# Attention and routed experts on one core: divisions one tile later, the clears begun by GpSimd, the last row cut six to two

## The chip, the cores and the metric

The kernel runs on one core of one Trainium2 chip. A core has five engines with a queue of instructions each: TensorE (PE; its weight loads are PEld in the profile), VectorE (DVE), ScalarE (ACT), GpSimd (POOL) and the sync engine (SP). DMA transfers are begun from such a queue and carried out by 16 DMA engines beside them. The metric is the device time of one execution in microseconds; the median of six executions is what counts.

## The reference

The input is `x` of 8 rows (batch entries) of 1024 tokens with 128 features, in float32. One layer with two residual steps is computed:

```
x = x + attention(layernorm(x)) @ Wo      # 16 heads of 8, each token sees the last 64 tokens
x = x + moe(layernorm(x)) + bias          # 8 experts of width 512, top 2, capacity 2048
```

The attention is a sliding window: token `l` attends to the tokens `l-63` to `l`, with a softmax over them. The second step routes each token to the two of 8 experts with the largest router probability. Each expert takes at most 2048 tokens in the order of the tokens, runs `gelu(t @ w1) @ w2` on them, and the result, times the router's probability, is added to the token's row.

## The kernel before

The work has two phases. **The first** (0 to about 493 us) does the attention, the norms and the routing, and writes each token's normalized features, its two probabilities, its first expert's code and its index into `xb`, a table in DRAM with 8 x 2048 slots of 132 words. **The second** (about 493 us to the end) loads each expert's slots (`load_e`), transposes them (L1283), multiplies by `w1` (L1294) and `w2` (L1305), scales (L1310) and adds the result to the output rows by an indirect DMA (L1315).

The first phase walks over 64 tiles, `i = 8 * b + j`: row `b` of 8, tile `j` of 8 with 128 tokens. In iteration `i` of the loop at L1165 the order of the code is: one clear of `xb` (below), `scores` of tile `i + 2`, what was left of the plan of tile `i - 1` (`behind`), `attend` of tile `i - 1`, `probs` of tile `i`, the plan of tile `i`, and the `late` steps of tile `i`. TensorE, VectorE, ScalarE and GpSimd run in this order, written by hand; the sync engine's order is set by the framework.

- `scores` (L526): TensorE makes the scores (L543, L559), VectorE takes their maxima over 768 columns (L567) and two differences (L575). The score buffers in PSUM are three, shared with `probs`, so a late L567 keeps TensorE from L604 or L612 of the next `probs`.
- `probs` (L591): scores again, transposed, with the maxima subtracted (L604 or, in the first tile of a row, L612; then L621, L628), then two exponentials on ScalarE (L634).
- `attend` (L640): the products with the values and, beside them, the sums of the exponentials (L649), copied out by ScalarE to `sums` (L657).
- `Context` (L662): sums and products of a group of tiles go from `sums` to the layout of the next product by DMAs on the sync queue: four for the divisors `den` (L678), four for `ctx` (L680). Then `scale` (L701) inverts the divisors of a tile (L706, VectorE) and multiplies (L707). `steps` says how many tiles after the copy each call runs. The groups of a row are tiles 0 to 3 (`few`: divisors inverted in a smaller layout through DRAM, L675 to L698, multiplied three tiles later), 4 to 5 and 6 to 7; in rows 6 and 7 they are pairs, and the last tile is alone.
- `Piece` (L752) is the rest of a token's way: `out` (projection by `Wo`, L783, residual L788, router logits L789), `stats` and `root` (layer norm, L377 to L405), `softmax`, `exp`, `apply`, `choose` 0 and 1 (top 2), `count` (two matmuls, L860), `place` (slot numbers, L872 to L881), `slots` (which hangs two scatters per tile into a list), and `keep` (adds the bias on GpSimd, L811, and stores the rows by the sync queue, L812).
- `put(n)` (L899) takes `n` scatters from that list: each is an indirect DMA begun by GpSimd (L905) that writes 128 rows of 528 bytes into `xb`.
- `first` (L926) does the first layer norm of a row two rows ahead; `turn`, `queries`, `keys`, `values` (L434 to L492) project the next row, and `spread` (L494) lays it out by DMAs.
- `clears` (L310): sixteen DMAs of 528 KB from a tile of zeros into `xb`, begun by the sync engine (L316), one in each of iterations 1 to 13 and then up to two, each behind the last matmul of `probs` of the tile before. The scatters come after all of them.

The plan (`at`, L921, the loop at L974 and `half`, L1023) says in which tile each step of a row's `Piece` and of the next rows runs. The routing of row `b - 1` runs during row `b`. Row 6 is cut into two pieces of four tiles. So is row 7 (`piece`, L1056): `go(ends[k], n)` runs the next `n` steps of a piece, after the loop mostly (L1222 to L1231). There, `mark` (L1234) is a small GpSimd instruction behind the scatters before the last five, and `stay_awake(38)` gives TensorE 38 matmuls that nobody reads (L169), begun after `mark`, until the second phase's first slots arrive.

## Time and profile before

| What | us |
|---|---|
| Median of 6 runs | 762.42 (760.38 to 768.49) |
| The profiled execution's own time | 758.78 |
| Its span, first to last instruction | 756.70 |
| First phase's loop, first L634 to 440.0 | 414.23, TensorE busy 354.93 |
| 440.0 to the first L1283 at 493.34 | 53.34, TensorE busy 16.14 |
| 493.34 to the end | 263.36, TensorE busy 240.64 |

The profile is that of one execution. The page gives, for each engine, its busy time, the chain of work that ended last, and the groups of instructions by source line, with their count, busy time, mean duration in ns and the idle time of the engine just before them, with what ended most of it. The trace behind it can be asked for stretches, waits and the order of time. In the order of time a line has: start, us, engine, line, operation, output and input, count, and in brackets the idle time before it with what ended it. `SPq` is the sync engine's queue: its time is the time to begin a DMA, not that of the transfer. In a table of stretches come start and end, length, the busy time of PE, PEld, DVE, ACT and POOL with their instructions, the granted TensorE clock as a share of full speed, the share of DMA time and GB/s.

### The profile page before, as it was taken

How to read it: one execution, taken by the hardware profiler on the slowest of the kernel's cores; microseconds unless marked ns; L12 is line 12 of the kernel's file. 1: busy time of each engine (PE TensorE's matmuls, PEld its weight loads, DVE VectorE, ACT ScalarE, POOL GpSimd, SP SyncE). 2: the span in 40 equal slices, each digit the busy share in tenths (PEclk: the TensorE clock that was granted, in tenths of full speed). 3: DMA queues.
4: the chain of work that ended last, by engine and by line, in shares of the span. 5: the costliest groups of instructions: out<-in, count | busy, mean ns of one | idle time of the engine just before them, and what ended most of it. 6: DMA issues, size and time to landing. Idle time of an engine off the chain costs nothing.

```text
span 756.7 us, 21773 instructions
## 1 busy us (share of the span) xinstructions
PE 633.4 (84%) x8777; PEld 469.7 (62%) x8777; DVE 393.3 (52%) x1229; ACT 363.1 (48%) x637; POOL 358.4 (47%) x353
## 2 busy tenths in 40 slices
PE   8898697899999989999977640599999999999990
PEld 6444454555556545555544430589999999898990
DVE  6675596797896978977889673221111111111010
ACT  5465367467666565665654520023444444443430
POOL 7000000133434334524414356548778787787876
PEclk9999899899999999999999875699999999999996
DMA  2544445333343434333332111246456365463333
GB/s 77 164 136 134 150 156 170 117 100 118 101 127 107 140 112 137 112 102 93 101 100 70 59 49 51 61 124 114 51 106 109 44 123 94 52 120 34 36 32 30
DMA packets 78307, 73.99 MB, mean 98 GB/s; under 512 B 13907, under 2 KB 63928, under 8 KB 77312
## 3 DMA queue, kind: packets, MB, share of 16 engines
q1 hardware_dynamic: 55296, 55.59, 23.1%
q0 software_dynamic: 22528, 16.74, 15.7%
q8 instruction: 69, 1.13, 0.7%
q14 instruction: 30, 0.25, 0.1%
q10 hardware_dynamic: 384, 0.28, 0.1%
HBM read 19.14 MB, written 30.28 MB: 65 GB/s over the span
## 4 chain that ended last, share of the span: by engine, by line
PE 43%; DVE 19%; ACT 10%; issue 9%; POOL 6%; SPq 5%; DMA 5%; another core or an unknown queue 0%; POOLq 0%; DVEq 0%; ACTq 0%
PE yp L1305 12%; PE hp L1294 12%; ACT pr L634 6%; DVE mx L567 5%; PE av L649 5%; POOL out_dram L1315 4%; PE t L621 4%; SPq L678 3%; ACT mxt L586 2%; DVE den L706 2%; DMA den<-sums 2%; PE xt L1283 2%; DMA ctx<-sums 1%; PE awake L169 1%; PE t L604 1%
## 5 line engine op out<-in xcount | busy, mean ns | idle before, releaser
L1315 POOL DMA_INDIRECT out_dram<-ye,dest x128 | 197.4, 1542 | 66.0 <-issue 27.7
L905 POOL DMA_INDIRECT xb<-xn,si x128 | 125.6, 981 | 212.0 <-PE s L559 61.8
L634 ACT ACTIVATE pr<-t 128x1024 f32<-128x1024 f32 x128 | 123.7, 1018 | 69.0 <-PE t L628 63.5
L1305 PEld LDWEIGHTS yp<-w,hT 128*128 128x128 f32 x1024 | 124.1, 192 | 8.4 <-ACT hT L1298 5.3
L1305 PE MATMUL yp<-w,hT 128*128 128x128 f32 x1024 | 125.3, 275 | 4.0 <-DVE ye L1310 3.3
L567 DVE TENSOR_REDUCE mx<-s 128x8 f32<-128x768 f32 x128 | 116.1, 949 | 15.9 <-PE s L559 15.9
L1294 PE MATMUL hp<-xts,w 128*128 128x256 f32 (+1 forms) x528 | 121.8, 373 | 0.3 <-DVE xts L1285 0.3
L1310 DVE TENSOR_TENSOR ye<-yp,gt 128x256 f32<-128x256 f32 (+1 forms) x66 | 27.1, 415 | 161.3 <-PE yp L1305 125.4
L1298 ACT ACTIVATE hT<-hp 128x512 f32<-128x512 f32 x128 | 76.3, 597 | 68.7 <-PE hp L1294 64.2
L1294 PEld LDWEIGHTS hp<-xts,w 128*128 128x128 f32 x528 | 93.3, 190 | 10.3 <-DVE xts L1285 0.6
L621 PE MATMUL t<-qbd,kt 32*128 32x256 f32 x1024 | 78.2, 397 | 0.0
L649 PE MATMUL av<-pr,vbd 128*32 128x128 f32 x2016 | 69.4, 278 | 8.2 <-ACT vbd L482 2.7
L657 ACT COPY sums<-av 128x512 f32<-128x512 f32 x63 | 36.9, 585 | 82.0 <-PE av L649 74.1
L811 POOL TENSOR_TENSOR x<-x,bias_sb 128x256 f32<-128x256 f32 x28 | 20.6, 750 | 113.2 <-ACT xn L417 113.0
L649 PEld LDWEIGHTS av<-pr,vbd 128*32 128x32 f32 x2016 | 52.1, 110 | 28.9 <-ACT mxt L586 13.3
L1285 ACT COPY xts<-xt 128x256 f32<-128x256 f32 (+1 forms) x57 | 21.0, 368 | 87.2 <-PE xt L1283 82.7
L559 PE MATMUL s<-kbd,qt 32*32 32x384 f32 x2048 | 59.9, 493 | 0.9 <-DMA kbd<-kt 0.9
L621 PEld LDWEIGHTS t<-qbd,kt 32*128 32x128 f32 x1024 | 54.5, 194 | 3.3 <-issue 1.6
L604 PE MATMUL t<-i,mt 32*128 32x256 bf16 x448 | 30.1, 277 | 17.0 <-DVE mx L567 15.5
L706 DVE RECIPROCAL den<-den 128x128 f32<-128x128 f32 x39 | 36.9, 947 | 12.7 <-DMA den<-sums 12.6
L586 ACT COPY mxt<-pm 128x512 bf16<-128x512 bf16 x64 | 37.8, 591 | 1.5 <-PE pm L584 1.5
L543 PE MATMUL s<-ms,i 32*128 32x256 bf16 x256 | 28.0, 276 | 11.4 <-ACT pr L634 6.4
(180 smaller groups left out, 730.4 us busy)
## 6 DMA issues: line engine op xcount, KB each, us to landing
xb<-zeros SPq DMA_DIRECT2D x16, 528.0 KB
xe<-xb SPq DMA_DIRECT2D x7, 1056.0 KB
vbd<-vbd SPq DMA_DIRECT2D x32, 192.0 KB
kbd<-kt SPq DMA_DIRECT2D x62, 72.0 KB
qbd<-qt SPq DMA_DIRECT2D x64, 64.0 KB
out_dram<-x SPq DMA_DIRECT2D x32, 128.0 KB
w<-in_L_ffn_w_dram SPq DMA_DIRECT2D x16, 256.0 KB
x<-in_L_attn_x_dram SPq DMA_DIRECT2D x22, 128.0 KB
```

What stands on the lines that cost most here:

```text
L559: done = nc.tensor.matmul(place(g, slice(32 * blk, 32 * (blk + 1))), lhsT=qt[quad(g), q0 : q0 + 32], rhs=kbd[quad(g), :, c0 + 32 * blk : c ...
L567: nc.vector.tensor_reduce(out=part_of(mx, 0)[:, 2 * u : 2 * u + 2], in_=units[u][:, :, 0 : 4 * KB].rearrange("p g (r k) -> p g r k", r=4), ...
L586: nc.scalar.copy(mxt.rearrange("p r w q -> p (r w q)"), pm.rearrange("p r q -> p (r q)"))
L621: nc.tensor.matmul(units[g // 2][:, g % 2, w], lhsT=kt[quad(g), q0 : q0 + P], rhs=qbd[quad(g), :, c0 : c0 + 64], start=False, stop=False, ...
L634: nc.scalar.activation(pr[:, 2 * u : 2 * u + 2], units[u], AF.Exp)
L649: last = nc.tensor.matmul(av[quad(g), k, :, w], lhsT=pair_values(vbd, 2 * j + w, g, k), rhs=pr[:, g, w, 2 * k : 2 * k + 2, :], start=True, ...
L706: nc.vector.reciprocal(den, den)
L905: ins = nc.gpsimd.indirect_dma_start(out=xb[:, :], out_offset=bass.IndirectOffsetOnAxis(ap=slot, axis=0), in_=row, in_offset=None, bounds_ ...
L1294: nc.tensor.matmul(hp[:, c], lhsT=ws[e][0][:, (c0 + c) * P : (c0 + c + 1) * P], rhs=xt, start=True, stop=True,)
L1298: nc.scalar.activation(hT[:, c0 : c0 + per], hp, AF.Gelu_apprx_tanh)
L1305: nc.tensor.matmul(yp[:, k, :], lhsT=hT[:, c, k * P : (k + 1) * P], rhs=ws[e][1][:, c, :], start=c == 0, stop=c == NC - 1,)
L1315: add = nc.gpsimd.indirect_dma_start(out=acc, out_offset=bass.IndirectOffsetOnAxis(ap=dests[e][:, n : n + 1], axis=0), in_=ye[:, k, :], in ...
```

## The change

The division of a tile (`scale`) runs two tiles after the copy for the first of a pair and three for the second, instead of one and two, and in rows 6 and 7 two for both. The steps that need it, and what follows them, move by a tile: the last projection, its statistics and root from tile 3 to 4, softmax to `place` from `n = b * NJ + 4` to `n = b * NJ + 5` on, while `slots` and the first `keep` stay in their tile. `values` of the next row goes from tile 4 to 5, behind `queries`; the statistics of the row after next from tile 1 to tile 7 of the row before. The last row's pieces have six and two tiles instead of four and four; the steps after the loop are shared out anew, and `mark` stands ahead of the last piece's `count`, `place` and `slots`. The sixteen clears are begun by GpSimd, from a tile of zeros of half the size, so with twice the runs of half the length.

```diff
-        zeros = c1.tile([P, 4, W], F32, tag="zeros", name="zeros")
+        zeros = c1.tile([P, 2, W], F32, tag="zeros", name="zeros")
...
-            n: c1.tile([P, E * n], F32, tag=f"goon{n}", name=f"go_on{n}") for n in (2, 4, 8)
+            n: c1.tile([P, E * n], F32, tag=f"goon{n}", name=f"go_on{n}") for n in (2, 4, 6, 8)
...
-                into = nc.sync.dma_start(
-                    out=to.rearrange("p (m k) -> p m k", m=NS // 8),
-                    in_=bc_mid(zeros.rearrange("p n d -> p (n d)"), NS // 8),
+                into = nc.gpsimd.dma_start(
+                    out=to.rearrange("p (m k) -> p m k", m=NS // 4),
+                    in_=bc_mid(zeros.rearrange("p n d -> p (n d)"), NS // 4),
                 )
...
-                return (
-                    (1 + t * (self.b != 6), partial(self.scale, t)) for t in range(self.n)
-                )
+                return ((2 + t * (self.b < 6), partial(self.scale, t)) for t in range(self.n))
...
-                at(b, 3, of, *f, "out", 6, 2)
+                at(b, 4, of, *f, "out", 6, 2)
             if b + 1 < B:
-                at(b, 4, values, b + 1, 0)
                 at(b, 4, turn, b + 1, 1)
                 at(b, 5, queries, b + 1, 1)
+                at(b, 5, values, b + 1, 0)
...
-                at(b, 1, first, b + 2, "stats")
+                at(b - 1, 7, first, b + 2, "stats")
...
-            at(b, 3, of, *f, "stats", range(2, 4))
-            at(b, 3, of, *f, "root", nc.vector)
-            n = b * NJ + 4
+            at(b, 4, of, *f, "stats", range(2, 4))
+            at(b, 4, of, *f, "root", nc.vector)
+            n = b * NJ + 5
             for t, what, *args in (
                 (n, "rooted"), (n, "softmax"),
                 (n + 1, "choose", 0),
                 (n + 2, "choose", 1),
-                (n + 5, "slots"),
-                (n + 5, "keep", (0,)), (n + 5, "keep", (2,)),
-                (n + 6, "keep", (4,)), (n + 7, "keep", (6,)),
+                (n + 4, "slots"),
+                (n + 4, "keep", (0,)), (n + 5, "keep", (2,)),
+                (n + 6, "keep", (4,)), (n + 6, "keep", (6,)),
...
-        half(6, 0, (53, 2), (54, 3), (56, 5), (57, 2), (58, 3))
-        half(6, 4, (57, 2), (58, 2), (59, 1), (60, 5), (61, 2), (62, 3))
+        half(6, 0, (53, 2), (55, 3), (56, 5), (57, 2), (58, 3))
+        half(6, 4, (57, 2), (59, 3), (60, 5), (61, 2), (62, 3))
...
-        ends = [piece(0, 4), piece(4, 8)]
+        ends = [piece(0, 6), piece(6, 8)]
         at(7, 5, go, ends[0], 2)
-        at(7, 7, go, ends[0], 8)
-        at(7, 7, go, ends[1], 2)
+        at(7, 7, go, ends[0], 9)
...
-        for which, n in ((0, 2), (1, 2), (0, 2)):
+        for which, n in ((0, 2), (1, 3), (0, 2)):
             go(ends[which], n)
         put(2)
         for n in (2, 1, 2):
             put(2, go(ends[1], n))
         put(len(puts), go(ends[1], 2))
+
+        mark = nc.gpsimd.memset(nothing, 0.0)
         go(ends[1], 3)
-        put(3)
+        put(len(puts))
         go(ends[0], 1)
         go(ends[1], 1)
-
-        put(max(0, len(puts) - 5))
-        mark = nc.gpsimd.memset(nothing, 0.0)
-        put(len(puts))
         after(stay_awake(38).ins, mark.ins)
```

## The prediction

> **What bounds the kernel now.** I read the page first, then a table of stretches cut where the first tile of each row begins its exponentials, then the list of waits, then the order of time around the two longest gaps and around the change of phase. The page gives three lines.

> ```profile
> PE 43%; DVE 19%; ACT 10%; issue 9%; POOL 6%; SPq 5%; DMA 5%; another core or an unknown queue 0%; POOLq 0%; DVEq 0%; ACTq 0%
> L706 DVE RECIPROCAL den<-den 128x128 f32<-128x128 f32 x39 | 36.9, 947 | 12.7 <-DMA den<-sums 12.6
> xb<-zeros SPq DMA_DIRECT2D x16, 528.0 KB
> ```

> The chain that ends last is TensorE's for less than half; VectorE, the sync queue and DMA hold 29% of it. VectorE stands idle before the division (L706) until the sums' DMA lands. The table of stretches (start:end, length, then busy time by engine) for rows 0, 1 and 3:

> ```profile
> 25.77:82.23 56.46, 45.63 (x892) 25.88 (x893) 34.75 (x97) 29.19 (x47) 0.00 (x0) 0.96 0.41 138
> 82.23:136.94 54.71, 45.78 (x864) 27.60 (x864) 39.45 (x120) 31.94 (x55) 1.49 (x2) 0.94 0.48 164
> 187.32:236.47 49.15, 44.82 (x867) 26.75 (x866) 40.62 (x123) 31.71 (x55) 18.66 (x20) 1.00 0.37 112
> ```

> TensorE is busy about 45 us in each. Rows 0 and 1 last 5 to 7 us longer, and GpSimd does next to nothing in them. By the starts of L634, the whole excess lies in one step: from the last tile of the row to the first of the next it takes 13.26 us (68.97 to 82.23) and 12.33 us (124.61 to 136.94), where rows 2 to 5 take 6.72, 6.73, 6.91 and 6.72. The order of time inside the first:

> ```profile
> 70.61 0.55 SPq L316 DMA_DIRECT2D xb<-zeros  x1
> 71.26 3.02 SPq L678 DMA_DIRECT2D den<-sums  x4
> 73.28 0.69 DVE L707 TENSOR_TENSOR ctx<-ctx,den 128x512 f32<-128x512 f32 x1 [4.61 <-DMA den<-one_910i]
> 74.32 2.50 SPq L680 DMA_DIRECT2D ctx<-sums  x4
> 75.55 0.95 DVE L706 RECIPROCAL den<-den 128x128 f32<-128x128 f32 x1 [1.58 <-DMA den<-sums]
> 78.14 0.29 DVE L707 TENSOR_TENSOR ctx<-ctx,den 128x128 f32<-128x128 f32 x1 [1.64 <-DMA ctx<-sums]
> 78.35 1.81 DVE L567 TENSOR_REDUCE mx<-s 128x8 f32<-128x768 f32 x2
> 79.36 0.51 PE L612 MATMUL t<-i,mt 32*128 32x128 bf16 x10 [6.61 <-DVE mx L567]
> 82.23 1.94 ACT L634 ACTIVATE pr<-t 128x1024 f32<-128x1024 f32 x2 [9.05 <-PE t L628]
> ```

> The maxima (L567) for scores made by 71.2 start at 78.35, because three VectorE instructions ahead of them wait for DMAs that the sync queue is late to issue: it has hardly a pause from 65 to 96 us. TensorE waits 6.61 us for those maxima, and its next matmuls run longer (16 of L621 in about 2.3 us instead of 1.1). The second gap is the same with 4.16 us at L612. So what ends last there is VectorE's order of work, not work.

> **The change, part by part.**

> *The division one tile later.* Its instructions stay: 39 times 0.95 us of L706 and 0.29 of L707. What goes is the wait in front of the maxima. In the gap above, the pair at 75.55 and 78.14 moves behind L567; what is late next is the 128x512 L707 of the row's first four tiles, whose lag doesn't change and whose divisors came at 73.28. The maxima would then start at 73.97 instead of 78.35, 4.4 us earlier; if that transfer comes before 71.2 the step falls to the other rows' 6.7. For 0-1 I take 7.8, a gain of 5.5, between 0 (the sync queue holds something else) and 6.5. For 1-2, where L707 ran at 129.17 against the pair's end at 133.2, I take 7.3, a gain of 5.0, between 0 and 5.6. Together 10.5 (0 to 12.1).

> In rows 2 to 5 the pair leaves a small wait: the step from tile 1 to tile 2 is 6.80, 6.67, 6.94 and 6.86 against 6.30, 5.51, 5.40 and 5.51 for the step before it, and in row 3 TensorE idles 0.84 us at L604 at 198.03 for a maximum behind an L707 that waited 1.52. I take 0.8 per row, 3.2 in all, between -1 (the pair lands on a busier tile) and 4.4 (1.1 each).

> *The steps moved with it.* The last output projection of a row (two L783 pairs, 0.73 us), its statistics and root (some 3 us of VectorE), softmax, choice, count and place go one tile later; the value projection goes from tile 4 to 5, with its four ACT copies and two vbd DMAs of some 0.65 us of sync issue; the next-but-one row's statistics (1.42 us) go from tile 1 to tile 7 of the row before. Nothing is added. VectorE is busy 40.6 of 49.15 us, so a tile has about 1 us free, and at tile 7 it waited 1.23 and 0.97 in row 3, which covers the statistics; without that cover they cost 1.4 per row. The input rows they read were issued by tile 5, one tile's notice. Zero in rows 2 to 5.

> Rows 6 and 7 are crowded. TensorE waits there for maxima 3.05 (395.01), 2.41 (416.11) and 3.20 us (424.33), each behind a string of routing steps and divisions. Two divisions (2.4 us) go from the string of tile 55 to that of tile 56, and one (1.2 us) from tile 59 to tile 60. Each moves the wait by 1.2 to 2.4 us and hardly removes it. I take 0, between a gain of 2 and a loss of 4.

> *The clears.* Sixteen issues of 0.56 us, 9 us in all, leave the sync queue, mostly in its unbroken stretch, and their wait for the tile's last matmul with them. I count this only as what lets the first L707 come earlier, as said. On GpSimd each becomes one transfer with 128x4 runs of half the length. No GpSimd transfer of this kind is in the trace; the nearest is a scatter (L905) of 128 runs at 0.97 us, so 0.97 to 4x0.97 = 3.9 us, and I take 2. GpSimd is idle in rows 0 and 1 (0.00 and 1.49 us busy), so even 62 us for the sixteen lies beside other work; behind them wait only the bias adds, from 114 us on, and the scatters, from row 2 on. The price that isn't covered is VectorE's: beside L811 on GpSimd at 411.45, L393 took 0.76 us instead of 0.17. But ten L905 between 443 and 455 left the VectorE instructions beside them at 0.16 to 0.2. I take 0; the upper end is the rival below.

> [...]

> *The change of phase.* Now it reads:

> ```profile
> 478.05 0.17 DVE L892 CAST si<-sl 128x8 int32<-128x8 f32 x1
> 478.97 1.09 POOL L905 DMA_INDIRECT xb<-xn,si  x1 [3.14 <-issue]
> 482.78 10.72 PE L169 MATMUL awake<-ident 128*128 128x128 f32 x76 [6.46 <-issue]
> 488.02 0.97 POOL L905 DMA_INDIRECT xb<-xn,si  x1 [0.30 <-issue]
> 490.37 2.25 SPq L1258 DMA_DIRECT2D xe<-xb  x5
> 493.34 0.38 PE L1283 MATMUL xt<-ident,xe 128*128 128x128 f32 x2
> ```

> The scatters cost 1.27 us each with the gap. Before, eight follow the last slots (478.22). After, the six-tile piece has twelve and the two-tile piece four; four of the twelve go after `choose` of the last piece, where GpSimd now idles 3.14 us, and only four remain behind the slots. Eight from about 476.1 end at 486.3 instead of 489.0, so the first load would land 2.7 us earlier, at about 490.6. But the 38 waking matmuls take 10.7 us from their mark, which now follows the first four: about 481.4 to 492.2. So TensorE begins at 492.2 instead of 493.34: 1.1 us. Ends: 2.9 gained, or 1 lost, since VectorE's instructions from 457.9 to 474.3 stand 0.5 to 1.4 us apart for a reason the trace doesn't name, and the last slots may come no earlier.

> *Not touched:* everything from 493.34 to the end (263.36 us, first by TensorE, at the end by GpSimd's scatters) moves as a block.

> **Sum.** 10.5 + 3.2 + 0 + 0 + 1.1 = 14.8 us. The profiled execution took 758.78 (span 756.70 and 2.08 around it), so it becomes 744.0. The median of the six runs is 762.42, 3.64 above; with the same distance 747.6, say 748.

> **The rivals.**

> - *Half (0.18).* The sync queue is the next bound: of the 31 us that it issues without a pause from 65 to 96, six clears are 3.4, so 28 stay, and with the step 5.5 shorter they would have to fit into 26. Then the two long steps come back by half (5 us), the rest gives 2 to 3: about 755. For it: that unbroken stretch. Against: rows 2 to 5 issue the same list in 49 to 51 us.
> - *More (0.12).* Rows 2 to 6 also even out: rows 2 to 5 last 50.0 us on average for 45.3 of TensorE; 48.5 each and 2 us in row 6 give 8 instead of 3.2: about 741.
> - *Nothing to measure (0.11).* The divisions arrive just when a maximum is due, in rows 6 and 7 with a loss of 4 and in rows 2 to 5 with 1, and the first rows give 5: 762.
> - *Slower (0.09).* [...] Place: sixteen tiles of rows 0 and 1. Price: up to 3.9 us each less 1 us free per tile, 16x2.9 = 46. From about 0.9 us net per clear it eats the 14.8. At 2.7 us each, 1.7 net, it is 27: about 775. For it: L393 above. Against: the ten scatters.
> - *The change doesn't take hold:* the other end of a division may be the last projection, not the maxima. It is in the third case.

> **How the numbers follow.** Forecast 0.50, around 748 (744 to 753). With half and more, 0.80 of the chance lies between 739 and 759; the cases left out are those of no change and slower. About 0.5% (3.8 us) is what a measurement of this kernel tells from no change, so faster means below 758.6: 0.80. Same 0.11, slower 0.09.

> **What would show it.** Right: the two long steps at 6.7 to 8 us and TensorE's waits for maxima at L612 gone from 12.6 us in total to below 4; no L707 with over 2 us of idle before it in rows 0 and 1; sixteen GpSimd transfers of 1 to 4 us; eight L905 in a row before the phase ends, and the waking matmuls starting near 12 us before the first L1283. Wrong: the steps still above 10 us with the sync queue still unbroken; VectorE instructions stretched beside the clears; or row 7 over 53 us.

## The result, and the profile after

The changed kernel takes 789.15 us (median of 20 runs, 783.93 to 793.43), the kernel before, beside it, 762.78 us (46 runs, 755.86 to 771.20). The ratio is 1.0337, 95% interval 1.0317 to 1.0357: **3.4% slower**, where 748 us was forecast. The profiled execution took 788.34 us, span 786.5.

The code moves by a few lines: in the changed kernel L903 is the scatter (L905 before), L781, L786 and L787 are the projection, residual and logits (L783, L788, L789), L858 is `count` (L860), L870 to L879 `place`, L1310 the last scatter (L1315), L1253 the load of slots (L1258).

The page's chain of the changed kernel, and two of its groups (busy us, mean ns, then the idle time before them):

```profile
PE 42%; issue 14%; DVE 13%; POOL 10%; ACT 8%; DMA 6%; SPq 5%; POOLq 0%; another core or an unknown queue 0%; DVEq 0%; ACTq 0%
L604 PE MATMUL t<-i,mt 32*128 32x256 bf16 x448 | 29.4, 292 | 31.0 <-DVE mx L567 29.1
L316 POOL DMA_DIRECT2D xb<-zeros x16 | 11.8, 742 | 90.0 <-PE pm L584 53.7
```

VectorE's share of the chain has gone from 19% to 13%, and L706, which idled 12.6 us for its divisors, now idles 0.8. But TensorE's wait for maxima at L604 has grown from 15.5 to 29.1 us, and "issue", time in which an engine waits for nothing that the profile names, from 9% to 14%. The clears take GpSimd 0.74 us each.

The table of stretches for rows 0, 1 and 3 of the changed kernel:

```profile
26.02:79.58 53.56, 45.62 (x892) 25.68 (x892) 34.84 (x99) 29.19 (x46) 6.04 (x8) 0.98 0.47 150
79.58:130.58 51.00, 46.18 (x863) 27.33 (x862) 38.20 (x114) 31.25 (x53) 6.47 (x9) 0.92 0.52 164
184.05:237.96 53.91, 45.44 (x867) 27.22 (x866) 41.13 (x123) 31.85 (x55) 18.62 (x20) 0.97 0.34 100
```

Rows 0 and 1 are 2.9 and 3.7 us shorter. Row 3 is 4.8 us longer with nearly the same work in it (TensorE busy 45.44 us, 44.82 before). The steps between the starts of L634 say where (mean of rows 2 to 5, us; two profiles of each kernel, the second ones from the experiments below, groups 3 and 5):

| step | before | before, again | changed | changed, again |
|---|---|---|---|---|
| tile 0 to 1 | 5.68 | 5.82 | **10.27** | **10.23** |
| 1 to 2 | 6.82 | 8.02 | 5.88 | 5.82 |
| 3 to 4 | 5.96 | 5.93 | 7.88 | 7.51 |
| 4 to 5 | 7.34 | 7.41 | 5.86 | 6.39 |
| 5 to 6 | 5.98 | 5.06 | 7.92 | 8.18 |
| 7 to the next row | 6.77 | 7.51 | 5.86 | 5.86 |
| the row | 50.02 | 50.83 | 55.01 | 55.82 |
| rows 0 and 1 together | 111.17 | 113.47 | 104.56 | 106.25 |
| row 7, last tile apart | 49.10 | 49.27 | 58.19 | 58.03 |

The forecast gain is there: the two row ends fell from 13.26 and 12.33 to 8.27 and 5.67. The order of time at the first of them:

```profile
75.28 0.69 DVE L707 TENSOR_TENSOR ctx<-ctx,den 128x512 f32<-128x512 f32 x1 [2.94 <-DMA den<-sums]
75.89 1.81 DVE L567 TENSOR_REDUCE mx<-s 128x8 f32<-128x768 f32 x2
76.90 0.40 PE L612 MATMUL t<-i,mt 32*128 32x128 bf16 x12 [1.81 <-DVE mx L567]
79.58 1.94 ACT L634 ACTIVATE pr<-t 128x1024 f32<-128x1024 f32 x2 [4.07 <-PE t L628]
```

The pair's division no longer stands ahead of L567; the 128x512 L707 does, as expected. What ate this is the step from tile 0 to tile 1. First row 3 before the change, then after it:

```profile
188.35 0.56 DVE L788 TENSOR_TENSOR x<-po,x 128x384 f32<-128x384 f32 x1 [1.18 <-PE po L783]
189.90 1.08 PE L649 MATMUL av<-pr,vbd 128*32 128x128 f32 x32
190.10 1.82 DVE L567 TENSOR_REDUCE mx<-s 128x8 f32<-128x768 f32 x2
```

```profile
184.13 0.43 PE L858 MATMUL pc<-both,lt 128*128 128x64 f32 x2
186.17 0.95 DVE L706 RECIPROCAL den<-den 128x128 f32<-128x128 f32 x1
186.20 1.20 PE L781 MATMUL po<-wo_sb,ctx 128*128 128x136 f32 x8
187.37 1.81 DVE L567 TENSOR_REDUCE mx<-s 128x8 f32<-128x768 f32 x2
189.55 0.55 DVE L786 TENSOR_TENSOR x<-po,x 128x384 f32<-128x384 f32 x1
190.29 1.94 PE L649 MATMUL av<-pr,vbd 128*32 128x128 f32 x32 [2.90 <-issue]
194.35 1.94 ACT L634 ACTIVATE pr<-t 128x1024 f32<-128x1024 f32 x2 [0.70 <-PE t L628]
```

Before, the residual (L788) of the first projection comes ahead of the maxima L567. After, its counterpart L786 comes behind them. The pool `ps_t` has two buffers in PSUM, the memory that this kernel's matmuls write to; `pm`, `pc`, the two `po` and `av` take them in turn: TensorE's L649 can't write `av` until L786 and L787 have read the first `po` (that L787 runs from 190.02 to 190.19, L649 starts at 190.29), so it stands 2.90 us, which the profile can only call "issue". The matmuls after it run slowly (L649 1.94 us instead of 1.08).

Why the order turned is one line of the loop that the diff doesn't touch: a tile's plan is cut at its second "product", and what stands from there on runs in the next iteration, behind the maxima.

```
n = [n for n, step in enumerate(plan[i]) if is_product(*step)][1:2]
```

Before, the products of tile 0 were `out(0,3)` and `out(3,1)`, so only the second slipped. With the routing one tile later `count`, which is also a product, lies in tile 0 and is the first; now both projections slip.

### The profile page after: what moved, and what is told of

It reads as the page before. It is cut to its first block, busy times and chain, and to the rows that moved or that the text cites. A ratio compares the mean times of both kernels' runs of the same rounds, so it can differ in the third digit from the quotient of the medians.

```text
span 786.5 us, 21778 instructions
## 1 busy us (share of the span) xinstructions
PE 643.4 (82%) x8777; PEld 475.3 (60%) x8777; DVE 392.8 (50%) x1229; ACT 364.5 (46%) x637; POOL 371.8 (47%) x371
## 4 chain that ended last, share of the span: by engine, by line
PE 42%; issue 14%; DVE 13%; POOL 10%; ACT 8%; DMA 6%; SPq 5%; POOLq 0%; another core or an unknown queue 0%; DVEq 0%; ACTq 0%
PE yp L1300 9%; PE hp L1289 9%; POOL out_dram L1310 6%; ACT pr L634 5%; PE av L649 5%; PE t L621 5%; DVE mx L567 3%; PE s L559 2%; DMA out_dram<-ye,dest 2%; POOL xb L903 2%; SPq L680 2%; PE t L604 2%; PE po L781 1%; PE awake L169 1%; ACT mxt L586 1%
## 5 line engine op out<-in xcount | busy, mean ns | idle before, releaser
L903 POOL DMA_INDIRECT xb<-xn,si x128 | 126.0, 984 | 233.8 <-PE t L628 74.4
L1310 POOL DMA_INDIRECT out_dram<-ye,dest x128 | 198.8, 1553 | 66.5 <-issue 28.3
L634 ACT ACTIVATE pr<-t 128x1024 f32<-128x1024 f32 x128 | 123.9, 1019 | 68.4 <-PE t L628 61.2
L567 DVE TENSOR_REDUCE mx<-s 128x8 f32<-128x768 f32 x128 | 116.3, 951 | 55.4 <-PE s L559 55.1
L649 PE MATMUL av<-pr,vbd 128*32 128x128 f32 x2016 | 71.4, 283 | 22.4 <-issue 15.3
L621 PE MATMUL t<-qbd,kt 32*128 32x256 f32 x1024 | 83.3, 424 | 0.4 <-issue 0.3
L657 ACT COPY sums<-av 128x512 f32<-128x512 f32 x63 | 36.9, 586 | 99.7 <-PE av L649 89.8
L649 PEld LDWEIGHTS av<-pr,vbd 128*32 128x32 f32 x2016 | 53.7, 112 | 48.1 <-issue 21.8
L621 PEld LDWEIGHTS t<-qbd,kt 32*128 32x128 f32 x1024 | 56.8, 208 | 5.6 <-issue 2.9
L604 PE MATMUL t<-i,mt 32*128 32x256 bf16 x448 | 29.4, 292 | 31.0 <-DVE mx L567 29.1
L316 POOL DMA_DIRECT2D xb<-zeros x16 | 11.8, 742 | 90.0 <-PE pm L584 53.7
L543 PE MATMUL s<-ms,i 32*128 32x256 bf16 x256 | 29.0, 281 | 12.6 <-ACT pr L634 9.2
L543 PEld LDWEIGHTS <-i 32*128 32x128 bf16 x256 | 10.0, 91 | 46.0 <-issue 41.6
## 6 DMA issues: line engine op xcount, KB each, us to landing
xb<-zeros POOLq DMA_DIRECT2D x16, 528.0 KB
```

The costliest lines, as they stand in the source:

```text
L567: nc.vector.tensor_reduce(out=part_of(mx, 0)[:, 2 * u : 2 * u + 2], in_=units[u][:, :, 0 : 4 * KB].rearrange("p g (r k) -> p g r k", r=4), ...
L604: nc.tensor.matmul(to, lhsT=mt[quad(g), 0, hq, :], rhs=i32[quad(g)].rearrange("p (w r) q -> p w r q", w=2), start=hq == 0, stop=False, ski ...
L621: nc.tensor.matmul(units[g // 2][:, g % 2, w], lhsT=kt[quad(g), q0 : q0 + P], rhs=qbd[quad(g), :, c0 : c0 + 64], start=False, stop=False, ...
L634: nc.scalar.activation(pr[:, 2 * u : 2 * u + 2], units[u], AF.Exp)
L649: last = nc.tensor.matmul(av[quad(g), k, :, w], lhsT=pair_values(vbd, 2 * j + w, g, k), rhs=pr[:, g, w, 2 * k : 2 * k + 2, :], start=True, ...
L903: ins = nc.gpsimd.indirect_dma_start(out=xb[:, :], out_offset=bass.IndirectOffsetOnAxis(ap=slot, axis=0), in_=row, in_offset=None, bounds_ ...
```

## The experiments

They ran in five groups, each on one chip with runs of the kernel before beside it; a ratio is to those. Comparisons of times are drawn within a group, because one program's ratio differed between two chips (1.0191 for `e12_sync` and 1.0263 for `e16_sync`, the last group). The one exception is the changed kernel's own time in the result, which groups 1 and 4 are held against.

**Group 1: the cut, the shift, the lag, the clears.** `e1_split` is the changed kernel with one edit:

```diff
-            n = [n for n, step in enumerate(plan[i]) if is_product(*step)][1:2]
+            cut = 2 if j == 0 and b > 1 else 1
+            n = [n for n, step in enumerate(plan[i]) if is_product(*step)][cut : cut + 1]
```

> The changed kernel with one edit: in the first tile of rows 2 to 7 the plan is cut ahead of its third product instead of its second, so the first output projection (L781 of tiles 0 to 2) and its two VectorE instructions run in that tile again, ahead of the next maxima. Theory S (the cut): `count` now stands first in that tile's plan and is counted as a product, so both projections fall behind the next tile's scores; TensorE's products with the values (L649) then wait for a PSUM buffer that VectorE frees only after L567. By it the step from tile 0 to tile 1 falls from 8.9, 10.3, 10.5, 11.4 and 10.4 us in rows 2 to 6 to about 6 each, 22 us less in all with row 7's part, and the time from 789 to about 767. Theory L (load: the moved divisions and routing steps are simply too much for VectorE in those tiles): the step stays above 9 us and the time above 784. Theory C (the clears on GpSimd disturb): the steps of rows 2 to 7 have no clears, so no change.

Measured: 772.60 us, ratio 1.0132 (1.0065 to 1.0200). The step from tile 0 to 1 is 6.7 to 6.8 in rows 2 to 6, and row 7 still takes 58.11. So the cut is the largest single cost that these experiments find, and not the only one.

`e2_shift` is the kernel before with the routing moved and nothing else:

```diff
-            n = b * NJ + 4
+            n = b * NJ + 5
...
-                (n + 5, "slots"),
-                (n + 5, "keep", (0,)), (n + 5, "keep", (2,)),
-                (n + 6, "keep", (4,)), (n + 7, "keep", (6,)),
+                (n + 4, "slots"),
+                (n + 4, "keep", (0,)), (n + 5, "keep", (2,)),
+                (n + 6, "keep", (4,)), (n + 6, "keep", (6,)),
```

> The kernel before with one part of the change alone: softmax, choice, count and place of a row one tile later, slots and keep where they end up after the change; divisions, clears and the last row as before. Theory S: the step from tile 0 to tile 1 of rows 2 to 7 grows by about 5 us each, as the count stands in that tile's plan: 762 + 6 x 5 = about 790 (range 780 to 795), with the long steps at the end of rows 0 and 1 still there. Theory L (it takes the divisions as well): under 770.

Measured: 791.55 us, 1.0381 (1.0312 to 1.0451). Tile 0 to 1 takes 8.8 to 11.0 in rows 2 to 7, and the long row ends stay (12.76, 13.64). Moving these steps alone is as bad as the whole change.

`e3_lag` is the kernel before with the divisions of rows 0 to 5 a tile later and, because they must follow, `out(6,2)`, its statistics and root in tile 4; `softmax` to `place` stay.

```diff
-                    (1 + t * (self.b != 6), partial(self.scale, t)) for t in range(self.n)
+                    (1 + (self.b < 6) + t * (self.b != 6), partial(self.scale, t))
+                    for t in range(self.n)
...
-                at(b, 3, of, *f, "out", 6, 2)
+                at(b, 4, of, *f, "out", 6, 2)
...
-            at(b, 3, of, *f, "stats", range(2, 4))
-            at(b, 3, of, *f, "root", nc.vector)
+            at(b, 4, of, *f, "stats", range(2, 4))
+            at(b, 4, of, *f, "root", nc.vector)
```

> The kernel before with the divisions of rows 0 to 5 one tile later, and with them the last projection, its statistics and root (tile 4 instead of 3); softmax to place stay in their tiles, so does everything of rows 6 and 7, the clears and the last row. Theory S with the prediction's own term: the steps from tile 7 to the next row fall from 13.3 and 12.3 us to about 7.5, those from tile 1 to 2 of rows 2 to 5 from 6.8 to 5.7: 10 + 4 less, and 2 us back in rows 2 to 5 at tile 3, where the moved division meets the norm's root: about 750 (744 to 755). Theory L: the moved divisions cost in rows 2 to 5 more than the first rows give: 762 or more.

Measured: 770.27 us, 1.0110 (1.0041 to 1.0178), a miss. The row ends fell (8.5, 6.75) and tile 1 to 2 went to 5.6 in rows 2 to 4 (6.4 in row 5), but the step from tile 4 to 5 rose to 9.6 to 9.9: projection, statistics, root and softmax now stand in one tile ahead of one L567. That string is the variant's own.

`e4_clears` is the kernel before with the clears alone changed (GpSimd, half the zeros, twice the runs).

> The kernel before with the clears alone changed: begun by GpSimd, from a tile of zeros of half the size. If they only unload the sync queue (nine us of issue in rows 0 and 1): the long steps of rows 0 and 1 become 1 to 3 us shorter each, 757 to 761. If they disturb (theory C, VectorE kept out or the DMA engines busier with runs of half the length): 765 or more. GpSimd's own instruction is 0.71 us each in the changed kernel.

Measured: 771.00 us, 1.0098 (1.0057 to 1.0139). The row ends did get shorter (11.40 and 6.75), but tile 5 to 6 of the same rows grew to 7.10 and 9.52. Beside the clears three small VectorE instructions are stretched by 0.1 to 0.25 us (L393 0.41 us instead of 0.17, L395 0.28 instead of 0.17, L412 0.47 instead of 0.34), and one, L851 at 124.79, beside a clear and two bias adds (L811), takes 1.80 instead of 0.23; the others keep their time. In its profile some 4 us of the loss is one step of row 4 (tile 1 to 2, 10.77), whose wait is for `ctx<-sums`, long after the clears. That wait led to the next group.

**Group 2: four edits on the kernel before.** `e5_pair`: the lag only where the long row ends need it.

```diff
-                    (1 + t * (self.b != 6), partial(self.scale, t)) for t in range(self.n)
+                    (1 + lag + t * (self.b != 6), partial(self.scale, t)) for t in range(self.n)
```

with `lag = self.b < 2 and self.j0 == 4`.

> The kernel before, and of the change only this: in rows 0 and 1 the two divisions of tiles 4 and 5 run one tile later. No routing step moves, the clears stay on the sync queue. Theory (the gain that was predicted exists and needs nothing else of the change): the two long row ends, 13.26 and 12.33 us, fall to between 7 and 9, the rest stays, and the time is 8 to 11 us below that of before, about 752. Rival (the division only hands the wait to the 128x512 L707 of tiles 0 to 3, since the sync queue with the clears in it is late with everything): the row ends stay above 10 us and the time is 757 to 762.

Measured: 1.0010 (0.9968 to 1.0052), a miss. The row ends did fall (8.60, 7.88); its profiled execution is one of its longest, with 8 to 14 us at tile 1 to 2 in rows 1 to 6, so that what took the gain can't be read from it.

`e6_cut`: only the cut, one earlier, so that `out(0,3)` slips as in the changed kernel.

```diff
-            n = [n for n, step in enumerate(plan[i]) if is_product(*step)][1:2]
+            cut = 0 if j == 0 and b > 1 else 1
+            n = [n for n, step in enumerate(plan[i]) if is_product(*step)][cut : cut + 1]
```

> The kernel before with one line changed: in tile 0 of rows 2 to 7 the plan is cut ahead of its first product instead of its second, so that out(0,3) as well as out(3,1) runs behind the next tile's maxima, as it does in the changed kernel. No routing step, division or clear moves. Theory (the cut): the step from tile 0 to tile 1 grows in rows 2 to 6 from 5.4 to between 8 and 10.5 us, TensorE waiting at L649 for the buffer that L788 reads behind L567; with row 7 the time is 15 to 28 us over that of before, 777 to 790. Rival (the extra time of the changed kernel's tile 0 is the work of count and place that has moved into it, not the place of out(0,3)): the step stays below 6.5 us and the time within 4 us of before.

Measured: 762.62 us, 1.0003 (0.9972 to 1.0034), against both the theory's time and the rival's step. The step from tile 0 to 1 did grow, to 7.9 to 9.4 in rows 2 to 6, but tile 1 to 2 fell to 5.6 to 6.0: the transfer that VectorE would have waited for there lands during the new wait. Here the delay cost nothing, because a later wait took it up.

`e7_short_sync` halves the clears' runs and leaves them on the sync engine; `e8_long_gpsimd` moves them to GpSimd with the old runs.

> The kernel before with the clears' source halved (2 instead of 4 rows of zeros), so that each clear has runs of half the length; the sync engine still begins them. Theory (GpSimd's queue is what the clears cost in the experiment with the clears alone, 771.0 against 761.5): no change, within 3 us of before. Rival (the shorter runs, or the shift of later buffers by 1 KB, cost it): 767 to 773.

> The kernel before with the clears begun by GpSimd but with runs of the old length (4 rows of zeros). Theory (GpSimd's queue): the same loss as with the halved runs, 767 to 773, of which 3 to 5 us lie behind the first xt (263 us before). Rival (the runs' length): within 3 us of before.

Measured: 1.0021 (0.9983 to 1.0060) and 1.0024 (0.9994 to 1.0054). Alone, the runs' length costs at most 0.6% and GpSimd's queue at most 0.5% here. `e4_clears`, which has both, was 1.0% slower on another chip; whether the two together or the chip made that difference, no run here tells. Both profiles have steps of 10 to 11 us from tile 1 to 2. One of them (row 3 of `e7_short_sync`), and below it the kernel before in row 4:

```profile
199.59 2.52 SPq L680 DMA_DIRECT2D ctx<-sums  x4
204.89 0.29 DVE L707 TENSOR_TENSOR ctx<-ctx,den 128x128 f32<-128x128 f32 x1 [3.08 <-DMA ctx<-sums]
206.11 0.61 PE L604 MATMUL t<-i,mt 32*128 32x256 bf16 x6 [3.99 <-DVE mx L567]
```

```profile
242.23 2.53 SPq L680 DMA_DIRECT2D ctx<-sums  x4
246.12 0.29 DVE L707 TENSOR_TENSOR ctx<-ctx,den 128x128 f32<-128x128 f32 x1 [1.51 <-DMA ctx<-sums]
```

The last of the four issues ends at 202.11 and 244.76; the data is there 2.8 us later in the one, 1.4 in the other.

**Group 3: before again, and a rows-only version.** `b2_before` is the kernel before, profiled once more.

> The kernel before, unchanged, profiled once more. Theory (the 1.1 us that a row's step from tile 1 to tile 2 had over its neighbours in the first profile is not a fixed price: the transfer ctx<-sums lands 1.3 to 3.1 us after its issue from one execution to the next, and the wait follows): in rows 1 to 6 at least three of these steps are above 8.5 us. Rival (the steps of 10 to 14 us in the last four profiles come from those edits): all six are between 6.6 and 7.9 us, as in the first profile.

Measured: 762.08 us. Steps from tile 1 to 2 in rows 1 to 6: 8.82, 7.05, 6.22, 11.43, 7.36, 8.26. Two above 8.5, not three, so the theory missed by one; but the rival's range, that of the first profile, is left too: the same program has 6.94 us in row 4 once and 11.43 the other time. The 1.1 us that the prediction read there was one execution's.

`e9_rows`: the changed kernel's plan for rows 0 to 5 with `e1_split`'s cut; rows 6 and 7, the clears and the end of the phase as before.

> The changed kernel's rows 0 to 5 (divisions one tile later, the routing and its statistics one tile later, the value projection in tile 5) with out(0,3) kept ahead of the maxima by a cut at the third product; rows 6 and 7, the clears and the end of the phase as before. Theory (the change's parts add up, and the two that hurt are the cut and rows 6 and 7): rows 0 to 6 as in the experiment with the cut mended (50.0 to 52.5 us each), row 7 near 50, the time 754 to 759, 0.5 to 1.2% under before. Rival (the routing string costs wherever it is put): 765 or more.

Measured: **753.30 us (752.53 to 753.94), 0.9906 (0.9876 to 0.9935)**, faster than both kernels. Rows 0 and 1 together take 102.88. Row 3 from tile 0 to 1 (L784, L789 are here projection and residual):

```profile
183.53 0.56 DVE L789 TENSOR_TENSOR x<-po,x 128x384 f32<-128x384 f32 x1 [0.29 <-PE po L784]
184.93 1.08 PE L649 MATMUL av<-pr,vbd 128*32 128x128 f32 x32
185.28 1.82 DVE L567 TENSOR_REDUCE mx<-s 128x8 f32<-128x768 f32 x2
```

The residual is ahead of the maxima again and L649 waits for nothing.

`e10_rows67` adds the changed kernel's rows 6 and 7 to it (the two lines below and the divisions two tiles behind the copy), `e11_tail` the changed end of the phase (with the clears' zeros halved for room).

```diff
-        half(6, 0, (53, 2), (54, 3), (56, 5), (57, 2), (58, 3))
-        half(6, 4, (57, 2), (58, 2), (59, 1), (60, 5), (61, 2), (62, 3))
+        half(6, 0, (53, 2), (55, 3), (56, 5), (57, 2), (58, 3))
+        half(6, 4, (57, 2), (59, 3), (60, 5), (61, 2), (62, 3))
```

> As the rows-only experiment of this batch, and on top of it the changed kernel's plan for rows 6 and 7 (their divisions two tiles behind the copy, the two halves' statistics later). Theory (the new strings of VectorE in row 7): row 7 goes from about 50 to 57 to 59 us, the time is 6 to 10 us above the rows-only experiment. Rival (row 7's length came from the other parts, the clears or the late end): row 7 below 53 and the time within 3 us of it.

> As the rows-only experiment of this batch, and on top of it the changed kernel's end of the phase (the last row in six and two, the waking matmuls from the earlier mark); for room in memory the clears' source is halved, still begun by the sync engine. Theory (as forecast: 1.1 us gained, between 2.9 gained and 1 lost): from the last L634 to the first xt within 3 us of the rows-only experiment and the time too. Rival (the six-tile piece lengthens the last strings of VectorE): 4 us or more above it.

Measured: 757.36 us, 0.9955 (0.9923 to 0.9987), 4.1 above `e9_rows`; and 755.07 us, 0.9935 (0.9908 to 0.9963), 1.8 above it. Row 7 went from 50.71 to 57.03 as expected, but row 6 from 53.80 to 50.37, which gave half of it back. In row 7 TensorE waits 6.42, 3.31, 1.43 and 4.82 us for maxima (6.41, 3.31, 1.51, 4.82 in the changed kernel, where the profile puts the third down to L398) instead of 3.75, 0.35, 3.31 and 3.20. The late end gains nothing: from the last L634 to the first xt it is 52.12 us against 51.29.

**Group 4: what the first three groups left open.** `e12_sync` is the changed kernel with `nc.gpsimd` put back to `nc.sync` in `clears`; `e13_gpsimd` is `e9_rows` with the changed clears; `e14_cut` is `e9_rows` with the loop's own cut; `e15_root` is `e9_rows` with

```diff
-                plan[b * NJ + 3].insert(0, (first, (b + 2, "root", nc.vector)))
-                plan[b * NJ + 3].insert(1, (first, (b + 2, "rooted")))
+                plan[b * NJ + 4].insert(0, (first, (b + 2, "root", nc.vector)))
+                plan[b * NJ + 4].insert(1, (first, (b + 2, "rooted")))
```

> The changed kernel with one word undone: the sync engine begins the clears (still in runs of half the length). Theory A (the clears on GpSimd cost what the traces show behind them, 2.2 us at the very end and 1 to 3 us around the change of phase): 784 to 787, and the span ends about 4.4 us after the last L1310 instead of 6.6. Theory B (they are the rest of the sum, 11 us): 776 to 780. The row ends of rows 0 and 1 tell besides what the clears are worth to the sync queue: if above 10 us again, the division's later tile alone was not what shortened them.

> The rows-only kernel with the clears on GpSimd, halved runs. Theory A: 3 to 6 us above the rows-only kernel's 0.9906, so a ratio of 0.994 to 0.999, with 2.2 us of it behind the last scatter. Theory B: 9 to 12 us, a ratio of 1.002 to 1.007.

> The rows-only kernel with the cut at the second product again, so that out(0,3) runs behind the maxima as in the changed kernel. Theory (the slip costs its full price once no later wait takes it up): the step from tile 0 to tile 1 goes from 6.7 to 10 to 11.5 us in rows 2 to 6, TensorE waiting 2.5 to 3.5 us at L649, and the time rises by 16 to 26 us to a ratio of 1.01 to 1.025. Rival (as in the kernel before, the slip is taken up elsewhere): within 4 us of the rows-only kernel.

> The rows-only kernel with the root of the next-but-one row's norm (some 3.5 us of VectorE) in tile 4 instead of tile 3. Theory (the moved division meets that root in tile 3, while VectorE then idles 2.7 us in tile 4 waiting for L784): the step from tile 3 to tile 4 falls from 7.1 to 8.9 to about 6, that from 4 to 5 rises by at most 1, and the time falls by 3 to 7 us, a ratio of 0.982 to 0.987. Rival (the string only moves on): within 2 us of the rows-only kernel.

| kernel | us | ratio |
|---|---|---|
| `e15_root` | 752.74 | 0.9894 (0.9843 to 0.9945) |
| `e13_gpsimd` | 758.73 | 0.9982 (0.9946 to 1.0018) |
| `e14_cut` | 768.65 | 1.0101 (1.0035 to 1.0168) |
| `e12_sync` | 774.38 | 1.0191 (1.0126 to 1.0255) |

`e14_cut` settles the contradiction of groups 1 and 2: where no later wait takes it up, the slip costs 15.9 us against `e15_root`. Tile 0 to 1 is 9.88, 9.80, 8.82, 10.95 and 8.82 in rows 2 to 6, 6.45 to 6.78 without the slip; these five steps alone make 14.8 of the 15.9 us. `e15_root` does the same as `e9_rows`: tile 3 to 4 fell to 5.07, which shows that the root met the moved division there, but tile 5 to 6 rose from 7.8 to 9.9. The string only moved on, as its rival said. `e13_gpsimd` lies 6.0 us above `e15_root`: theory A. `e12_sync` spoke for theory B: 774.38, where the changed kernel had 789.15, but not beside it.

**Group 5: the clears in the changed kernel, on one chip.** `b3_after` is the changed kernel, `e16_sync` the same program as `e12_sync`.

> The changed kernel, unaltered, on the same chip as the next. Theory A (the clears cost the same here as in the rows-only kernel, about 6 us, and the rest of the difference was the chip): 5 to 8 us above the kernel with the clears on the sync engine. Theory B (they cost more here): 11 to 15 us above it, and the traces differ in the rows, not only behind them.

> The changed kernel with the clears begun by the sync engine, once more, beside the changed kernel on one chip. Theory A: 5 to 8 us below it. Theory B: 11 to 15 us below it.

Measured: 787.93 us, 1.0284 (1.0209 to 1.0359), and 785.47 us, 1.0263 (1.0194 to 1.0331). The difference is 2.5 us, less than either theory; with four runs of each, 783.67 to 793.63 and 783.67 to 786.87, it isn't clear of the noise. Theory B falls: `e12_sync` and `e16_sync` are one program, and take 774.38 on one chip and 785.47 on the other. What the clears cost in every profile is at the end of the program; the last scatter of the changed kernel (span 786.5) and of `e16_sync` (span 784.8):

```profile
778.31 1.55 POOL L1310 DMA_INDIRECT out_dram<-ye,dest  x1 [0.30 <-issue]
```

```profile
778.99 1.54 POOL L1310 DMA_INDIRECT out_dram<-ye,dest  x1 [0.30 <-issue]
```

From its end to the end of the span it is 6.6 us with the clears on GpSimd and 4.3 without. The stretch from the first xt to the end is 266.1 to 268.5 us in the five profiles with halved clears on GpSimd, and 263.0 to 265.1 in all with them on the sync engine.

## Why the prediction was wrong, point by point

1. **The division one tile later (-10.5, 0 to 12.1): right.** Rows 0 and 1 went from 113.47 (`b2_before`) to 102.88 in `e9_rows`, 10.6 less. In the changed kernel it is 6.6 (111.17 to 104.56). The gain varies with the execution: the kernels with all of these divisions later take 102.8 to 106.8 in their profiles, those with none of them 110.1 to 114.9. TensorE's waits for maxima at L612 fell from 12.6 us to 3.0, as forecast, though the 128x512 L707 still waited 2.94 us in row 0. The clears on GpSimd brought a wait that the prediction didn't have: L690, the inversion of the few divisors, waits 3.65 us (at 63.37) and 3.69 (at 114.17) for `one<-total`, and tile 5 to 6 takes 7.17 and 11.66 us instead of 5.06 and 5.41. On one chip it is 7.22 and 11.48 with those clears, 5.65 and 9.46 without. The two rows together gain nothing from the sync engine, though: 104.85 and 105.65 in `e12_sync` and `e16_sync`. Nor do the short row ends need GpSimd: `e12_sync` has 8.10 and 5.12.
2. **Tile 1 to 2 in rows 2 to 5 (-3.2): right.** It is 0.9 us a row against the first profile, where 0.8 was forecast, and 2.1 against the second.
3. **The steps moved with it: the step that failed.** The prediction said: "Nothing is added. VectorE is busy 40.6 of 49.15 us, so a tile has about 1 us free", and put "Zero in rows 2 to 5". It counted instructions and VectorE's room. But the plan's order is also cut by a rule over its products, and moving `count` changed which call is cut off, so that L649 stood 2.9 to 3.4 us in each of rows 2 to 6: 15.9 us (`e14_cut` against `e15_root`), and 791.55 us where this shift was the only edit. A smaller part is strings: division and root at tile 3 to 4, softmax and L412 at tile 5 to 6, about 2 us each in rows 2 to 5, given back at 1 to 2, 4 to 5 and 7 to 0 (rows 2 to 5 take 51.04 on average in `e9_rows`, 50.02 and 50.83 before).
4. **Rows 6 and 7 (0, -2 to +4): at the end of its range**, +4.1 (`e10_rows67`). The sign of error that it named, row 7 over 53 us, came true (58.19).
5. **The clears (0): the stretched VectorE instructions that it feared came once, and small.** They take 0.74 us each instead of the estimated 2. In the changed kernel VectorE is held up beside one of the sixteen: L393, at 108.42, and L395 behind it end with the clear begun at 108.14, after 0.43 and 0.31 us, where the same two take 0.16 and 0.17 in the next row; the string comes 0.16 us later by it. In this trace all of GpSimd's idle time ahead of the clears ends by TensorE (90.0 us: 53.7 by L584, 36.3 by L628), as the order asks, and none by VectorE. The cost is 6.0 us in the rows-only kernel and 2.5, not clear of the noise, in the changed one; 2.3 of it lies behind the last scatter, where the prediction said that all "moves as a block".
6. **The change of phase (-1.1, -2.9 to +1): +1.8 (`e11_tail`), outside its range.** Only four scatters were left behind the mark, as forecast (the last at 513.60), but the last L634 to the first xt took 56.11 us instead of 55.74: the waking matmuls ran from 509.60 to 520.58 and TensorE's first xt, at 520.42, came with their end.

So the way from 761.37 (before, in group 4) to the 774.38 of `e12_sync` is -8.6 for the rows (`e15_root`), +15.9 for the cut (`e14_cut`) and +5.7 for rows 6 and 7 and the end, for which group 3 has 4.1 and 1.8. With 2.5 to 6.0 for the clears the changed kernel should take 777 to 780 on that chip, where it wasn't run. What it took elsewhere, 788 to 789, holds another 8 to 12 us that no part of the change explains by itself: the program with the clears on the sync engine is 13.0 us above before in group 4 and 21.4 in group 5. Its two profiled executions are 12.6 us apart, of which 4.2 lie in tile 0 to 1 of rows 2 to 6 and 6.4 between the last L634 and the first xt. The next section shows both places; why the chips differ there stays open.

No rival had the mechanism. "Slower" had the sign with another cause; its price (VectorE held up beside the clears, by the author's estimate up to 2.9 us each) was paid once, with 0.16 us, and no run shows the whole of it. The rival "more" was added up wrong besides: 748 less the 4.8 us that it gains is 743, not 741.

## What to carry to other kernels

When a step of a hand-written order is moved, list the order that results on each engine, with every rule that cuts or sorts it, before pricing the step at nothing: here the moved instructions cost little, and the call that they pushed behind the next maxima cost 16 us. The "issue" wait of TensorE in front of a matmul that starts a new PSUM tile (2.90 us at L649) was here a buffer not yet read out, by an instruction that stood late in VectorE's order; the profile doesn't name it. One profile is one execution: a step that ended by a DMA took 6.94 us once and 11.43 the next time, and an edit's cost can be hidden by such a wait (`e6_cut`) or stand alone (`e14_cut`).

## What the runs showed of the hardware

**Whether a wait of TensorE of 2 to 3 us costs a slow stretch after it depends on where it falls.** The same step of row 4 in one program on two chips, `e16_sync` and then `e12_sync` (the stretch from the start of L649 to the next L634; the granted clock is the third number from the end):

```profile
246.27:250.48 4.21, 4.21 (x63) 2.80 (x64) 1.97 (x7) 1.36 (x3) 0.00 (x0) 0.59 0.10 27
```

```profile
244.96:247.55 2.59, 2.59 (x63) 1.90 (x64) 1.98 (x7) 1.36 (x4) 0.00 (x0) 1.00 0.17 50
```

TensorE had idled 2.92 and 2.89 us. After it, the granted clock is 0.59 in the one and 1.00 in the other, and the same 63 matmuls take 4.21 and 2.59 us. In rows 2 to 6 of `e16_sync` L649 ran 1.54 to 1.94 us after every such wait, in `e12_sync` 1.08 in four of five. In `e6_cut` it happened in row 6 after only 1.96 us (L621 1.92 us), in rows 3 and 4 not.

```profile
243.33:246.74 3.41, 0.49 (x19) 0.50 (x22) 3.31 (x11) 0.00 (x0) 0.32 (x1) 1.00 0.36 105
```

```profile
239.98:243.39 3.41, 2.09 (x42) 1.23 (x40) 3.30 (x9) 1.16 (x2) 0.97 (x1) 1.00 0.68 176
243.39:246.81 3.42, 1.85 (x52) 1.63 (x56) 3.19 (x11) 0.71 (x2) 0.00 (x0) 1.00 0.27 81
```

Counted over all twenty traces from 30 to 440 us: of the stretches at full clock with TensorE busy for under 40%, all 112 were followed by half clock; of those with 40 to 60%, 73 of 151; of those with more, 1 of 1844. In `e6_cut` the stretch ahead of row 6's slow one (348.60 to 352.01) had 1.45 us busy of 3.41, or 42%. Such a stretch need not be idle: in the kernel before TensorE was busy for 1.18 us of the 3.42 from 422.09 to 425.51, or 35%, and the clock was half from 425.51 on.

These slow stretches are not all of the difference between the two executions: from 30 us to the last L634 the clock was half for 51 us in `e16_sync` and for 72 in `e12_sync`, the faster one.

**VectorE's small instructions can stand apart.** At the end of the first phase the instructions from L405 to L849 of the last piece take 3.8 us in `e12_sync` (479.35 to 483.19) and 14.7 in `e16_sync` (489.00 to 503.69), most of them starting 0.5 to 2.1 us after the one before, with scatters at 1.28 us distance on GpSimd beside them in both. From the last L634 to the first xt it is 52.3 and 58.8 us. In all kernels of groups 1 and 5 this stretch takes 55.6 to 58.8 us, in those of groups 2 to 4 50.1 to 53.4. No run here says what sets it. As it goes by groups, and a group has one chip, the chip is the likelier ground, but that isn't shown.

**A plain GpSimd transfer** of 528 KB took its engine 0.71 us in the changed kernel (median of sixteen, 0.69 in `e8_long_gpsimd` with runs of twice the length), less than the scatter of 128 rows (0.98). With the sixteen begun there instead of by the sync engine, the span ended 1.5 (long runs, `e8_long_gpsimd`) to 2.3 us later behind the last scatter.
